# Three-layer graph convolution: comparisons for the count products made five at a time and earlier, more places for count products and matrices, shared chunk rows split once per group

## The chip, the cores and the metric

The kernel runs on one core of a Trainium2 chip. The time is the device time of one execution in microseconds (us). The profile comes from a hardware profiler that recorded one execution of its own. Engines are named as in the profile: PE (TensorE, matrix products; PEld is its loading of the stationary operand), DVE (VectorE), ACT (ScalarE), POOL (GpSimd, which here issues the gathers), SP (SyncE, which issues most other transfers).

## The reference

A graph of 6250 nodes with 256 features and 100000 edges, sorted by destination, goes through three graph convolutions, then a residual sum and a normalisation. Biases are drawn at random, and W1 is scaled by 8. Widths are 256 to 512, 512 to 512 and 512 to 256.

```python
def _gcn_layer(h_in, W, b, src, dst, norm_edge, n_nodes):
    h = h_in @ W
    msg = h[src] * norm_edge[:, None]
    agg = jax.ops.segment_sum(msg, dst, num_segments=n_nodes)
    return agg + b
...
src = jnp.concatenate([edge_index[0], loops])
dst = jnp.concatenate([edge_index[1], loops])
deg = jax.ops.segment_sum(jnp.ones_like(dst, dtype=x.dtype), dst, num_segments=n)
dinv = jnp.where(deg > 0, jax.lax.rsqrt(deg), 0.0)
norm_edge = dinv[src] * dinv[dst]
h = x
for W, b in ((W1, b1), (W2, b2), (W3, b3)):
    h = jax.nn.relu(_gcn_layer(h, W, b, src, dst, norm_edge, n))
return h
...
x = _layernorm(x + _L0_gnn_ref(x, edge_index, ...), axis=-1)
```

All is float32.

## The kernel before

**Blocks, chunks and groups.** The nodes are cut into 50 blocks of Q = 125. A block's incoming edges are taken as KF = 16 *chunks* of 128 edges; what a block has beyond 2048 edges goes into a *shared chunk*, one for each group of GRP = 10 blocks. The sum over edges into a node is done in one of two ways.

*Gathered blocks.* For each chunk an indirect DMA, issued by POOL (L829), brings the 128 source rows from a table in DRAM into a row buffer in `room`. DVE makes a one-hot matrix `shot` (L798; four chunks at a time, by comparing `near_cols`, the numbers 0 to 124 in a PSUM bank, with the edges' destinations), and PE multiplies the two into the block's accumulator `sacc` (L855). Where a chunk is *halved*, its float32 row is first split into a high part (ACT, L870) and a remainder (DVE, L873), `halves`, and goes through PE as one product in the mode float32r; where it is not, it goes as float32. Halved are every second chunk in layer 0, three of four in layer 1, and all in layer 2, but never the shared chunk. The shared chunk's rows are gathered once in a group, and multiplied once for each block, after its sixteenth chunk.

*Dense blocks.* For the first FEW = 18 blocks in layer 0 and the first MANY = 28 in layer 2, no rows are gathered. A matrix of counts (how many edges from each node into each of the block's nodes, one byte each, 125 x 6250) is loaded from the DRAM tensor `kept` into one of two places `used`, widened into `piece` five source blocks at a time (L806), and 50 products with `parts`, the split features of all nodes held in SBUF, give the same sum (L898).

**Counting.** The count matrices are themselves made on the chip by `counts(b)` (L688), 18 in layer 0 and ten in layer 1. It goes through 28 steps; a count product handles G = 5 destination nodes, so there are GB = 25 in a block and 700 in all. For each, DVE compares the numbers in `keys` with one column of `slots` twice: `hot_lo` (L702) marks an edge's place in its source block, `hot_key` (L704) its source block and destination node. Two steps later PE multiplies them into one half of the PSUM tile `mat_ps`, the half alternating (L710), and a step after that ACT copies the counts as bytes into `made` (L694). After the last copy SP stores `made` to `kept` (L713), and there is one `made`:

```python
if u > 2:
    moved(u - 3)
if 1 < u < GB + 2:
    hot_lo, hot_key = hot.pop(u - 2)
    nc.tensor.matmul(mat_ps[:Q, u % 2, :G * NB], lhsT=hot_lo, rhs=hot_key, start=True, stop=True)
if u % rush != rush - 1:
    yield 1
```

`slots` comes from `windows(t)` (L429), six rounds of small products and comparisons, two of them before layer 0.

**Order of the work.** The instructions of each engine run in the order in which the program writes them; waits between engines follow from the tiles that they share, a tile of a pool being taken as a whole. Each layer is a loop over the chunks (L864). One step issues the gather of chunk c, the high split of chunk c - hi_lag, the remainder of c - lo_lag and the product of c - lag, then lets everything else move on by one step: first what finishes a block (`after1`, `after2`, `after3`: scaling, transposing, weight products, bias, relu, store), then `go_fixed` (L877), which advances windows and counting, then as many dense products as an even spread asks for. The lags are in L37:

```python
SPLIT = ((1, 2, 4), (1, 2, 4), (3, 4, 6))
```

A gather may run ahead of its product by as many steps as there are row buffers: of `first_rows` two are kept for shared chunks and 19 rotate in layer 0. Layer 0 has 516 gathers (32 blocks and four groups' shared chunks), layer 1 has 805, layer 2 355. `making_few` (L1059) runs the counting of layer 0: it counts a block, then, when the dense block before the last is finished, fetches the block's matrix into `used`, then counts the next. In layer 1 the ten countings start at fixed, evenly spread chunks. Pools of `halves` have three buffers in layer 0 and four in layers 1 and 2; `pairs`, which holds the hot tiles, has four.

## Time and profile before

| | us |
|---|---|
| median of three executions | 2779.82 |
| lowest and highest | 2773.82, 2794.70 |
| the profiled execution, and its span in the records | 2769.12, 2767.1 |
| clock granted to PE, mean over the span | 0.905 |

The largest groups of instructions, from the page (line, engine, what, how often, busy us, mean ns):

| line | engine and work | count | busy | mean |
|---|---|---|---|---|
| L829 | POOL, gather issue | 1664 | 1650.0 | 992 |
| L855 | PE, gathered product, halved rows | 1808 | 773.3 | 486 |
| L855 | PE, gathered product, unsplit rows | 1120 | 483.9 | 516 |
| L898 | PE, dense product (three places of the sum) | 2300 | 765.0 | |
| L710 | PE, count product | 700 | 203.4 | 291 |
| L873 | DVE, remainder of a split | 1208 | 663.6 | 556 |
| L798 | DVE, `shot` | 443 | 296.3 | 669 |
| L702, L704 | DVE, comparisons | 1400 | 401.7 | 277, 297 |
| L870 | ACT, high part of a split | 1208 | 600.9 | 510 |
| L694 | ACT, copy of counts | 700 | 305.6 | 437 |
| L806 | ACT, `piece` | 376 | 264.9 | 712 |

How to read what is shown further on: the page's first part gives busy time, share of the span and number of instructions per engine; its slices cut the span into 40 parts and give busy tenths; its chain follows the work that ended last back to the start, and "issue" is time in which an engine waited for nothing that the records show. In the view by stage a row begins with the stretch in us from the start of the span. In the view of waits a row names an engine, the tile and line of the instruction that waited, what it is taken to have waited for, then total us, times and the longest. In the timeline a row is start, duration, engine, line and operation with out<-in, and in brackets the idle time ahead of it and what ended it. Records on one engine can overlap, and busy PE time is not PE at its peak.

### The profile page before, as it was taken

How to read it: one execution, taken by the hardware profiler on the slowest of the kernel's cores; microseconds unless marked ns; L12 is line 12 of the kernel's file. 1: busy time of each engine (PE TensorE's matmuls, PEld its weight loads, DVE VectorE, ACT ScalarE, POOL GpSimd, SP SyncE). 2: the span in 40 equal slices, each digit the busy share in tenths (PEclk: the TensorE clock that was granted, in tenths of full speed). 3: DMA queues.
4: the chain of work that ended last, by engine and by line, in shares of the span. 5: the costliest groups of instructions: out<-in, count | busy, mean ns of one | idle time of the engine just before them, and what ended most of it. 6: DMA issues, size and time to landing. Idle time of an engine off the chain costs nothing.

```text
span 2767.1 us, 30455 instructions
## 1 busy us (share of the span) xinstructions
PE 2130.1 (77%) x7965; PEld 1459.2 (53%) x7965; DVE 1512.0 (55%) x3904; ACT 1266.9 (46%) x2777; POOL 1685.0 (61%) x1717
## 2 busy tenths in 40 slices
PE   3367678887878767878778878778787688888886
PEld 2245445555555434545555545545454466666664
DVE  5555445555555355555555555555554255655656
ACT  2445445555555344444444444444444244444443
POOL 2355556666666466667767667676676366566663
PEclk9988889999999888989998889999899789999998
DMA  7344445455445466666767667676676355555553
GB/s 174 92 124 115 134 136 146 123 149 148 126 143 143 123 196 194 203 195 201 211 191 211 186 181 216 195 203 201 182 216 198 98 137 150 142 147 153 151 145 93
DMA packets 178089, 447.70 MB, mean 162 GB/s; under 512 B 43347, under 2 KB 75429, under 8 KB 177904
## 3 DMA queue, kind: packets, MB, share of 16 engines
q0 software_dynamic: 107456, 326.24, 42.1%
q1 hardware_dynamic: 55328, 107.63, 13.5%
q10 hardware_dynamic: 15120, 11.77, 1.7%
q8 instruction: 65, 1.06, 0.2%
q14 instruction: 120, 0.98, 0.1%
HBM read 391.61 MB, written 53.88 MB: 161 GB/s over the span
## 4 chain that ended last, share of the span: by engine, by line
PE 53%; issue 17%; DVE 9%; another core or an unknown queue 7%; ACT 6%; DMA 5%; POOL 3%; ACTq 0%; POOLq 0%; SPq 0%; DVEq 0%
PE sacc L855 20%; PE sacc L898 10%; PE win_ps L985 5%; DMA room<-tab,ssrc 4%; PE win_ps L898 4%; PE mat_ps L898 3%; PE mat_ps L710 3%; PE smm L945 3%; DVE halves L873 3%; ACT halves L870 3%; POOL room L829 2%; PE smm L1002 2%; DVE shot L798 1%; ACT piece L806 1%
## 5 line engine op out<-in xcount | busy, mean ns | idle before, releaser
L829 POOL DMA_INDIRECT room<-tab,ssrc x1664 | 1650.0, 992 | 878.8 <-issue 333.3
L873 DVE TENSOR_TENSOR halves<-room,halves 128x256 fp32r<-128x256 f32 (+1 forms) x1208 | 663.6, 556 | 805.1 <-ACT halves L870 382.7
L855 PE MATMUL sacc<-halves,shot 128*125 128x512 f32 x1808 | 773.3, 486 | 156.0 <-issue 66.0
L870 ACT CAST halves<-room 128x256 fp32r<-128x256 f32 (+1 forms) x1208 | 600.9, 510 | 610.9 <-PE sacc L855 170.0
L855 PEld LDWEIGHTS sacc<-halves,shot 128*125 128x125 f32 x1808 | 349.4, 203 | 494.1 <-issue 289.1
L694 ACT CAST room<-mat_ps 125x250 uint8<-125x250 f32 x700 | 305.6, 437 | 544.2 <-PE mat_ps L710 165.4
L898 PE MATMUL sacc<-parts,piece 125*125 125x512 f32 x1400 | 498.7, 454 | 34.5 <-ACT piece L806 19.4
L855 PE MATMUL sacc<-room,shot 128*125 128x256 f32 (+1 forms) x1120 | 483.9, 516 | 10.6 <-DMA room<-tab,ssrc 10.6
L710 PE MATMUL mat_ps<-hot_key,hot_lo 128*125 128x250 bf16 x700 | 203.4, 291 | 308.3 <-issue 128.5
L898 PEld LDWEIGHTS sacc<-parts,piece 125*125 125x125 f32 x1400 | 254.8, 203 | 274.0 <-issue 196.4
L702 DVE TENSOR_SCALAR hot_lo<-keys,slots 128x125 bf16<-128x125 bf16 x700 | 193.6, 277 | 264.9 <-remote 114.2
L798 DVE TENSOR_TENSOR shot<-near_cols,sdlo 128x500 fp32r<-128x500 f32 x443 | 296.3, 669 | 0.1
L806 ACT CAST piece<-room 125x625 fp32r<-125x625 uint8 x376 | 264.9, 712 | 59.5 <-DVE halves L873 13.0
L855 PEld LDWEIGHTS sacc<-room,shot 128*125 128x125 f32 x1120 | 218.7, 204 | 130.0 <-issue 69.8
L985 PE MATMUL win_ps<-room,w_sb 128*128 128x250 f32 x800 | 218.2, 399 | 6.0 <-ACT room L993 5.3
L704 DVE TENSOR_SCALAR hot_key<-keys,slots 128x250 bf16<-128x250 bf16 x700 | 208.1, 297 | 0.0
L985 PEld LDWEIGHTS win_ps<-room,w_sb 128*128 128x128 f32 x800 | 164.7, 206 | 58.1 <-issue 26.1
L898 PE MATMUL mat_ps<-parts,piece 125*125 125x512 f32 x450 | 132.2, 412 | 16.9 <-ACT piece L806 8.4
L898 PE MATMUL win_ps<-parts,piece 125*125 125x512 f32 x450 | 134.1, 419 | 13.5 <-ACT piece L806 10.3
L710 PEld LDWEIGHTS <-hot_lo 128*125 128x125 bf16 x700 | 104.5, 150 | 60.9 <-issue 24.2
L945 PE MATMUL smm<-w,szt 128*125 128x512 f32 x200 | 110.6, 641 | 1.3 <-DVE st L950 0.6
L1002 PE MATMUL smm<-w,room 128*125 128x256 f32 x400 | 109.0, 398 | 0.0
(174 smaller groups left out, 1246.8 us busy)
## 6 DMA issues: line engine op xcount, KB each, us to landing
room<-kept SPq DMA_DIRECT2D x46, 683.6 KB
room<-tab,ssrc POOLq DMA_INDIRECT x1664
kept<-room SPq DMA_DIRECT2D x28, 683.6 KB
tab<-st SPq DMA_DIRECT2D x75, 224.0 KB
room<-tab SPq DMA_DIRECT2D x50, 224.0 KB
room<-in_x SPq DMA_DIRECT2D x50, 112.0 KB
out<-st ACTq DMA_DIRECT2D x50, 112.0 KB
room<-in_x ACTq DMA_DIRECT2D x4, 1120.0 KB
```

The costliest lines, as they stand in the source:

```text
L694: nc.scalar.copy(made[:, :, u * G:(u + 1) * G], mat_ps[:Q, u % 2, :G * NB].rearrange("p (k r) -> p k r", r=G))
L704: nc.vector.tensor_scalar(hot_key, keys, slots[:, t, 1, w:w + 1], None, op0=ALU.is_equal)
L710: nc.tensor.matmul(mat_ps[:Q, u % 2, :G * NB], lhsT=hot_lo, rhs=hot_key, start=True, stop=True)
L798: nc.vector.tensor_tensor(hot[:, :n], near_cols.unsqueeze(1).to_broadcast([P, n, Q]), dlo.rearrange("p b j -> p (b j)")[:, at:at + n].unsq ...
L806: convert(piece, used[m % 2][:, c * PIECE:(c + 1) * PIECE, :])
L829: nc.gpsimd.indirect_dma_start(out=row, out_offset=None, in_=tables[i], in_offset=bass.IndirectOffsetOnAxis(ap=at, axis=0))
L855: nc.tensor.matmul(acc[:Q, :size], lhsT=hot, rhs=row[:, c0:c0 + size], start=(i == 1 and k == c0 == 0), stop=(k == KF and c0 + size == row ...
L870: nc.scalar.copy(halves[:, :width], landed[chunk - hi_lag])
L873: nc.vector.tensor_sub(halves[:, width:], landed.pop(chunk - lo_lag), halves[:, :width].bitcast(F32))
L898: nc.tensor.matmul(acc_d[:Q], lhsT=got[done // PIECE][:, k % PIECE, :], rhs=parts[:, k], start=False, stop=(k == NB - 1))
L945: nc.tensor.matmul(y_ps, lhsT=zt[:, k, :], rhs=w1_sb[:, k, :], start=(k == 0), stop=(k == KC - 1))
L985: nc.tensor.matmul(h_ps[:, f, :], lhsT=w2_sb[:, k, (f2 + f) * P:(f2 + f + 1) * P], rhs=zt2[:, k, :], start=(k == 0), stop=(k == KH - 1))
```

## The change

- **Comparisons.** `counts` takes a list of blocks and makes the comparisons of WIDE = 5 count products together: one TENSOR_TENSOR for five `hot_lo` and two for five `hot_key` (three columns at one step, two columns two steps later). They read `near_cols`, which now holds the numbers 0 to 249 in float32, and `slots`, now BF16, each spread by broadcasting. `pairs` holds two tiles of five.
- **Count products.** A product comes four steps after the step that starts its five, its copy one step later. Products go in turn to three places: the two halves of `mat_ps`, and columns 256 to 505 of the PSUM bank that also holds `near_cols`.
- **Matrices.** Counting of layer 0 runs on without a break between blocks, 25 steps a block, and fills `made` and a second place `also_made` in turn; the first block still goes at about two products a step. Fetching is a list of steps of its own, and takes a block once its store has been issued. In layer 1 each count of a block has the one place `made`, as before. `also_made` takes the room of six row buffers: 13 rotate in layer 0.
- **Shared chunk.** Its row is split like a halved chunk, once for its group, into a pool of its own with two buffers, and all blocks of the group use these halves.
- **Sizes.** `halves` has four buffers in layer 0 and five in layer 2. `dynamic_dma_scratch_size` is 4096. `thr0` is dropped (`windows` computes it from `cols`), and b3 is loaded between layers 1 and 2, on SP, into a tile made there, rather than before layer 0.

The diff, without the lines that move b3 and without what is unchanged:

```diff
-    slots = const.tile([P, NW, 2, Q], F32, name="slots")
+    slots = const.tile([P, NW, 2, Q], BF16, name="slots")
...
     cols = const.tile([P, P], F32, name="scols")
-    thr0 = const.tile([P, Q], F32, name="thr0")
...
         thr = scratch[:P, 0:125]
-        nc.vector.tensor_single_scalar(thr, thr0, float(G * Q * t), op=ALU.add)
+        nc.vector.tensor_scalar(thr, cols[:, :Q], float(G), float(G * Q * t), op0=ALU.mult, op1=ALU.add)
...
-    made, *used = [room[:Q, n * MW:(n + 1) * MW].bitcast(U8)[:, :NB * Q].rearrange("p (k v) -> p k v", v=Q) for n in range(3)]
-    first_rows = [room[:, at:at + C] for at in range(3 * MW, room.shape[1] - C + 1, C)]
+    made, *used, also_made = [room[:Q, n * MW:(n + 1) * MW].bitcast(U8)[:, :NB * Q].rearrange("p (k v) -> p k v", v=Q)
+                              for n in range(4)]
+    first_rows = [room[:, at:at + C] for at in range(4 * MW, room.shape[1] - C + 1, C)]
...
-    pairs = early.enter_context(tc.tile_pool(name="spairs", bufs=4))
+    pairs = early.enter_context(tc.tile_pool(name="spairs", bufs=2))
...
-    split = one.enter_context(tc.tile_pool(name="sfirst_split", bufs=3))
+    split = one.enter_context(tc.tile_pool(name="sfirst_split", bufs=4))
+    shared_split = one.enter_context(tc.tile_pool(name="sfirst_shared", bufs=2))
...
-    near_cols = ps_cols.tile([P, 512], F32, name="near_cols")[:, :Q]
-    nc.vector.tensor_copy(near_cols, cols[:, :Q])
+    near = ps_cols.tile([P, 512], F32, name="near_cols")
+    near_cols = near[:, :G * NB]
+    nc.vector.tensor_copy(near_cols, keys)
+    mat_places = [mat_ps[:Q, 0, :G * NB], mat_ps[:Q, 1, :G * NB], near[:Q, 256:256 + G * NB]]
...
-    def counts(b, rush=GB + 3):
-        def moved(u):
-            nc.scalar.copy(made[:, :, u * G:(u + 1) * G],
-                           mat_ps[:Q, u % 2, :G * NB].rearrange("p (k r) -> p k r", r=G))
+    def counts(blocks, places, rush=0):
+        def compared(out, numbers):
+            shape = list(out.shape)
+            nc.vector.tensor_tensor(out, near_cols[:, :shape[2]].unsqueeze(1).to_broadcast(shape),
+                                    numbers.unsqueeze(2).to_broadcast(shape), op=ALU.is_equal)
         hot = {}
-        for u in range(GB + 3):
-            if u < GB:
-                t, w = divmod(b * GB + u, Q)
-                hot_lo = pairs.tile([P, Q], BF16, name="hot_lo")
-                nc.vector.tensor_scalar(hot_lo, hot_cols[:, :Q], slots[:, t, 0, w:w + 1], None, op0=ALU.is_equal)
-                hot_key = pairs.tile([P, G * NB], BF16, name="hot_key")
-                nc.vector.tensor_scalar(hot_key, keys, slots[:, t, 1, w:w + 1], None, op0=ALU.is_equal)
-                hot[u] = hot_lo, hot_key
-            if u > 2:
-                moved(u - 3)
-            if 1 < u < GB + 2:
-                hot_lo, hot_key = hot.pop(u - 2)
-                nc.tensor.matmul(mat_ps[:Q, u % 2, :G * NB], lhsT=hot_lo, rhs=hot_key, start=True, stop=True)
-            if u % rush != rush - 1:
+        total = len(blocks) * GB
+        for s in range(total + 5):
+            if s < total and s % GB == 0:
+                while (blocks[s // GB] + 1) * GB > seen * Q:
+                    yield 1
+            if s < total and s % WIDE == 0:
+                t, w = divmod(blocks[s // GB] * GB + s % GB, Q)
+                hot_lo = pairs.tile([P, WIDE, Q], BF16, name="hot_lo")
+                hot_key = pairs.tile([P, WIDE, G * NB], BF16, name="hot_key")
+                hot[s // WIDE] = hot_lo, hot_key
+                compared(hot_lo, slots[:, t, 0, w:w + WIDE])
+                compared(hot_key[:, :3], slots[:, t, 1, w:w + 3])
+            if s < total and s % WIDE == 2:
+                t, w = divmod(blocks[s // GB] * GB + s % GB + 1, Q)
+                compared(hot[s // WIDE][1][:, 3:], slots[:, t, 1, w:w + WIDE - 3])
+            m = s - 4
+            if 0 <= m < total:
+                hot_lo, hot_key = [h[:, m % WIDE] for h in hot[m // WIDE]]
+                nc.tensor.matmul(mat_places[m % 3], lhsT=hot_lo, rhs=hot_key, start=True, stop=True)
+            m = s - 5
+            if 0 <= m:
+                n, u = divmod(m, GB)
+                place = places[n % len(places)]
+                nc.scalar.copy(place[:, :, u * G:(u + 1) * G], mat_places[m % 3].rearrange("p (k r) -> p k r", r=G))
+                if u == GB - 1:
+                    by_rows(nc.sync, place.rearrange("p k v -> p (k v)"), kept[blocks[n]], store=True)
+                    stored.append(blocks[n])
+            if s >= rush or s % 2:
                 yield 1
-        by_rows(nc.sync, made.rearrange("p k v -> p (k v)"), kept[b], store=True)
     there = []
     finished = 0
+    stored = []
     def fetch(b, chunk):
         by_rows(nc.sync, used[len(there) % 2].rearrange("p k v -> p (k v)"), kept[b])
         there.append(chunk)
-    hot_cols = keys
...
                 hot = onehot.tile([P, HOTS, Q], F32R, name="shot")
-                nc.vector.tensor_tensor(hot[:, :n], near_cols.unsqueeze(1).to_broadcast([P, n, Q]),
+                nc.vector.tensor_tensor(hot[:, :n], near_cols[:, :Q].unsqueeze(1).to_broadcast([P, n, Q]),
...
         landed, split_rows = {}, {}
+        group_rows = None
...
         def halved(c):
-            return 0 <= c < total and items[c][1] is not None and (i == 2 or items[c][2] % (2, 4)[i] > 0)
+            return 0 <= c < total and (items[c][1] is None or i == 2 or items[c][2] % (2, 4)[i] > 0)
...
                 row, at = shared[n % 2], rest[:, n, 0:1]
             else:
                 row, at = rows[turn % len(rows)], src[:, b, j:j + 1]
-                landed[c] = row
                 turn += 1
+            landed[c] = row
...
         def product(c):
             nonlocal acc
+            nonlocal group_rows
             n, b, j = items[c]
             if b is None:
+                group_rows = split_rows.pop(c)
                 return
...
             several = [(j, split_rows.pop(c) if halved(c) else landed.pop(c))]
             if j == KF - 1:
-                several.append((KF, shared[b // GRP % 2]))
+                several.append((KF, group_rows))
...
                 if halved(chunk - hi_lag):
-                    halves = split_rows[chunk - hi_lag] = split.tile([P, 2 * width], F32R, name="halves")
+                    pool, name = (split, "halves") if items[chunk - hi_lag][1] is not None else (shared_split, "shared")
+                    halves = split_rows[chunk - hi_lag] = pool.tile([P, 2 * width], F32R, name=name)
                     nc.scalar.copy(halves[:, :width], landed[chunk - hi_lag])
...
-    def making_few():
+    def fetching_few():
         for m, b in enumerate(few):
-            while (b + 1) * GB > seen * Q:
-                yield 1
-            yield from counts(b) if m else counts(b, 2)
-            while finished < m - 1:
+            while b not in stored or finished < m - 1:
                 yield 1
             fetch(b, now + 10)
     first = 28
     spacing = (steps(FEW) - first - 12) / FEW
-    layer(0, C, every[FEW:], few, after1, first_rows, first, spacing, [(0, all_windows()), (1, making_few())])
+    layer(0, C, every[FEW:], few, after1, first_rows, first, spacing, [(0, all_windows()), (1, counts(few, (made, also_made), GB)), (1, fetching_few())])
...
     split = two.enter_context(tc.tile_pool(name="swide_split", bufs=4))
+    shared_split = two.enter_context(tc.tile_pool(name="swide_shared", bufs=2))
...
-          extras=[(5, last_weights())] + [(10 + gap * n, counts(b)) for n, b in enumerate(many[FEW:])])
+          extras=[(5, last_weights())] + [(10 + gap * n, counts([b], (made,))) for n, b in enumerate(many[FEW:])])
...
-    split = ctx.enter_context(tc.tile_pool(name="ssplit", bufs=4))
+    split = ctx.enter_context(tc.tile_pool(name="ssplit", bufs=5))
+    shared_split = ctx.enter_context(tc.tile_pool(name="sshared", bufs=2))
...
-    nc = bacc.Bacc("TRN2", target_bir_lowering=False, num_devices=1)
+    nc = bacc.Bacc("TRN2", target_bir_lowering=False, num_devices=1, dynamic_dma_scratch_size=4096)
```

## The prediction

> **What bounds the kernel now.** I read the page first (engines, slices, chain), then busy time by stage, then who waited for whom in each stage, and last a stretch of the timeline.
>
> ```profile
> PE 2130.1 (77%) x7965; PEld 1459.2 (53%) x7965; DVE 1512.0 (55%) x3904; ACT 1266.9 (46%) x2777; POOL 1685.0 (61%) x1717
> ...
> PEclk9988889999999888989998889999899789999998
> ...
> PE 53%; issue 17%; DVE 9%; another core or an unknown queue 7%; ACT 6%; DMA 5%; POOL 3%; ACTq 0%; POOLq 0%; SPq 0%; DVEq 0%
> ```
>
> The reader is to see that TensorE (PE) is the busiest engine and more than half of the chain, but idle for 637 us, and that a quarter of the chain is nobody's work ("issue", "unknown queue"). The clock row never stays at full speed: it falls after idle stretches. By stage:
>
> ```profile
> core 0: us, PE busy (x) PEld busy (x) DVE busy (x) ACT busy (x) POOL busy (x), PEclk, DMA share, GB/s
> 0.00:100.00 100.00, 32.47 (x197) 26.14 (x197) 55.71 (x138) 34.60 (x64) 18.89 (x38) 1.00 0.64 157
> 100.00:931.00 831.00, 639.28 (x2528) 444.56 (x2529) 434.60 (x1460) 423.69 (x1025) 501.01 (x520) 0.90 0.46 132
> 931.00:953.00 22.00, 13.44 (x45) 7.06 (x43) 7.41 (x15) 6.49 (x15) 0.46 (x1) 1.00 0.23 71
> 953.00:2190.00 1237.00, 965.28 (x3352) 621.01 (x3353) 679.49 (x1414) 540.25 (x1077) 823.14 (x810) 0.89 0.68 195
> 2190.00:2767.00 577.00, 479.61 (x1845) 360.43 (x1844) 334.75 (x878) 261.87 (x597) 341.48 (x351) 0.91 0.52 138
> ```
>
> The stages are preparation, layer 0 (516 gathers, so 1.61 us a step), a handover, layer 1 (805, 1.54 us) and layer 2 (355, 1.63 us). In layer 0 PE idles 192 us. The waits of PE in 100 to 931 us (total us, times, longest):
>
> ```profile
> PE mat_ps L710 <- issue: 60.8, 30, 6.9
> PE mat_ps L710 <- DVE hot_key L704: 53.5, 26, 13.8
> PE mat_ps L710 <- ACT room L694: 45.0, 31, 5.9
> PE mat_ps L710 <- DVE hot_lo L702: 15.6, 16, 3.0
> ```
>
> Nearly all of it, 174.9 us in 103 waits, stands ahead of one instruction, the count product L710. In 953 to 2190 us the same line has 67.7 + 21.8 + 21.7 + 5.2 + 4.2 = 120.6 us. Whom the tool names differs, but the program's waits are plain: each L710 waits for the L694 copy of the product just before it (`mat_ps` is tracked as one tile, so its two halves do not help), and that copy waits for that product. PE to ACT and back, once a step. The timeline shows what this does:
>
> ```profile
> 218.78 0.37 PE L710 MATMUL mat_ps<-hot_key,hot_lo 128*125 128x250 bf16 x1 [2.01 <-issue]
> ...
> 223.93 0.44 ACT L694 CAST room<-mat_ps 125x250 uint8<-125x250 f32 x1 [4.63 <-remote]
> 223.93 0.34 DVE L702 TENSOR_SCALAR hot_lo<-keys,slots 128x125 bf16<-128x125 bf16 x1 [5.18 <-remote]
> ...
> 224.42 0.37 PE L710 MATMUL mat_ps<-hot_key,hot_lo 128*125 128x250 bf16 x1 [3.99 <-ACT room L694]
> ```
>
> The product at 218.78 lasts 0.37 us, yet its copy and a comparison that waits for it both start at 223.93: PE's answer came 4.8 us late. Why, the trace does not say; whatever has no slack pays for it in full. A second cause: there is one `made`, so the first copy of a block waits until the last block's store has landed. ACT's waits in layer 0:
>
> ```profile
> ACT room L694 <- remote: 106.2, 24, 12.9
> ...
> ACT room L694 <- DMA kept<-room: 40.2, 10, 5.5
> ```
>
> Ten are named, 4.0 us each; there are 17 such block changes.
>
> **The change, part by part.** The sum is against the profiled execution (span 2767.1, 2769.1 us); the median of the runs shown is 10.7 us above it, added at the end.
>
> (a) Shared rows split once. 54 products in layers 0 and 2 were two f32 passes of 408 ns each and become one of 486: 54 × 330 ns = 17.8 us. 50 in layer 1 were 2 × 651 and become 2 × 486: 16.5 us. Added are 12 splits (ACT 404 or 618 ns, DVE 423 or 691), beside idle ACT and DVE. On the path I count layers 0 and 2 in full and half of layer 1: **−26**.
>
> (b) `also_made`. The 17 waits vanish in layer 0, about 3 us of PE idle each (4.0 less what PE still had): **−50**. SP's stores and loads are as many as before.
>
> (c) Products and copies. In the new program the two products into `mat_ps` wait for copies two and three products back (one wait serves both); the third, in the `near` bank, for the copy three back. Slack goes from one step to two or three. Left of L710's waits is 125 us in layer 0, mean 1.7 us; two more steps are 2.5 us of PE work (639/516 = 1.24 us a step), so most of a wait is covered. But late answers come in rows, and one product in three hangs on DVE (f). I take half in layer 0, **−62**. In layer 1 half is 60, and POOL presses there (823 busy + 810 × 0.30 us between gathers = 1066 of 1237), so **−40**. Counting also takes 25 steps a block instead of 28, which spreads dense products; no further gain taken.
>
> (d) Comparisons. Five columns were ten TENSOR_SCALAR; now three TENSOR_TENSOR of 625, 750 and 500 elements, reading `near_cols` in PSUM. From the subtraction rows (256: 423 ns, 512: 691 ns) an element is 1.05 ns and the rest 155 ns: 809 + 940 + 670 (the measured `shot` of 500) = 2.42 us. Before, by rows, 5 × (277 + 297) = 2.87 us, but the records overlap:
>
> ```profile
> 205.51 0.25 DVE L702 TENSOR_SCALAR hot_lo<-keys,slots 128x125 bf16<-128x125 bf16 x1
> 205.68 0.27 DVE L704 TENSOR_SCALAR hot_key<-keys,slots 128x250 bf16<-128x250 bf16 x1
> ...
> 205.88 0.24 DVE L702 TENSOR_SCALAR hot_lo<-keys,slots 128x125 bf16<-128x125 bf16 x1
> ```
>
> 0.37 us a pair, 1.85 us for five; the new three with 0.1 us of overlap each make 2.13. So over 140 fives −63 to +39 us of DVE. [...]
>
> (e) Layer 2 gets five `halves` instead of four. Its ACT splits wait 68.0 + 30.0 + 25.9 + 16.9 us for PE, and PE 36.1 us for DVE `halves` in turn: **−20**. Layer 0's fourth goes with (c). Fewer idle stretches also keep the clock up: layer 0 at 0.90 has about 20% of its time at half speed, and a quarter of that saved over 639 us of work is some 15 us: **−15**.
>
> (f) New waits. `near_cols` and the third place are one tile. So each third product waits for the last DVE read of it (a `shot` or comparison), and the next DVE read waits for that product and its copy; behind the waiting DVE stand the `halves` subtractions that PE wants. No row shows it. Round trip per three products: product 0.3 + copy 0.44 + gaps 0.3, and up to two steps of DVE at 435/516 = 0.84 us, in bad places a 1.75 us pair plus about 1.7 us more: 2.7 to 4.5 us, against 3 × 1.24 = 3.7 of PE work. Bounds: 0, and 0.8 us for all 233 round trips, 186 us. By the DVE load nearer the low end: **+35**.
>
> (g) Layer 0's rotating rows fall from 19 to 13, so gathers run nine steps ahead of their product instead of fifteen: some 11 to 14 us. The longest gather wait in layer 0 is 7.9 us. Between 0 and 30: **+10**. [...] BF16 `slots`, the dropped `thr0` and the late `b3` are a handful of instructions and one DMA on SP at the start of layer 2, ahead of a first use several steps later: zero.
>
> Sum: −26 − 50 − 62 − 40 − 20 − 15 + 35 + 10 = −168; 2769 − 168 + 11 = **2612 us**.
>
> **Rivals.** *Late answers pass through.* If PE's answers come late in rows and the third place hands them on, (c) and the clock fail: 2780 − 26 − 50 − 20 + 45 = 2729. For it: clusters, as between 213 and 232 us. Against: most waits are under 2.5 us.
> *The shared bank decides (slower).* If the round trip PE, ACT, DVE, PE of (f) takes longer than three steps of today, 3 × 1.61 = 4.83 us, layer 0 gains nothing. At 5.8 us its 150 trips cost +145, less 26 and 20: 2780 + 99 = 2879. For it: a comparison pair of 1.75 us in one step. Against: DVE's 0.84 us a step.
> *All slack is found.* L710's waits go almost entirely, and layer 2 follows: −26 − 55 − 110 − 85 − 30 − 25 + 30 = −301, about 2480. For it: L710 is nearly PE's only wait in layer 0. Against: gathers alone, at 1.25 us each, need 645 us of layer 0.
>
> **How the numbers follow.** Forecast 0.66 (2550 to 2690), pass-through 0.14, shared bank 0.08, all slack 0.12. The range 2530 to 2755 leaves out the slow case, half of the fastest and a few hundredths of the rest, some 0.19. Within 1% of 2780 (2752 to 2808) is about what a measurement of this kernel cannot tell from no change. Faster: 0.66 + 0.12 + most of 0.14, less the forecast's tail, 0.85; same 0.06; slower 0.09.
>
> **What would show it.** In the new profile: PE's idle before the count product in layer 0 well under 100 us, with few `kept` stores among ACT's waits; layer 0 near 720 us, layer 1 near 1190, layer 2 near 550; unsplit products gone from layer 2; gathers as long as now. Wrong would be: long waits of DVE's reads of `near_cols` or of each third product, or POOL waiting for rows while ACT waits for landings.

## The result and the profile after

The changed kernel took 2753.06 us (four runs, 2749.66 to 2761.23) beside 2784.90 us for the kernel before: a ratio of 0.987, 95% interval 0.9827 to 0.9913. It is faster beyond its interval, but by 32 us, where 168 were forecast. Repeated beside the kernel before on two more occasions it gave 0.9829 (0.9805 to 0.9852) and 0.9851 (0.9818 to 0.9884).

One thing has to be known to read what follows. The runs went to several chips of the same type, and these fall into two kinds. On kind A (the first comparison and two later sets of runs) the kernel before takes 2785 to 2796 us; on kind B (three sets, each on a chip of its own) it takes 2351 to 2353 us. Each kernel was timed beside the kernel before on the same chip, so ratios hold; microseconds are compared only within a kind. On kind B the changed kernel is slower: 1.0074 (1.005 to 1.0098).

From the page of the changed kernel (first comparison, kind A), engines, clock and chain:

```profile
PE 2108.5 (76%) x7911; PEld 1444.9 (52%) x7911; DVE 1544.8 (56%) x2935; ACT 1247.0 (45%) x2789; POOL 1683.6 (61%) x1716
...
PEclk9889999999998788998998998889889789999998
...
PE 38%; issue 15%; DVE 8%; ACT 7%; another core or an unknown queue 7%; DMA 4%; POOL 1%; SPq 1%; ACTq 0%; DVEq 0%; POOLq 0%
```

The view by stage, cut here at the first and last gather of each layer (columns as in the prediction), shows layers 0, 1 and 2:

```profile
core 0: us, PE busy (x) PEld busy (x) DVE busy (x) ACT busy (x) POOL busy (x), PEclk, DMA share, GB/s
...
98.70:896.40 797.70, 621.62 (x2507) 427.39 (x2508) 457.24 (x840) 412.64 (x1035) 504.40 (x519) 0.92 0.48 138
...
918.20:2137.10 1218.90, 943.50 (x3272) 606.58 (x3272) 687.02 (x1057) 530.73 (x1067) 814.65 (x805) 0.88 0.67 195
...
2171.30:2733.80 562.50, 464.45 (x1796) 356.16 (x1797) 319.80 (x841) 252.31 (x582) 345.27 (x354) 0.91 0.53 141
```

Cut in the same way, the kernel before had 833.4, 1197.3 and 558.4 us. So layer 0 gave 36 us and the other two gave nothing; their differences are those of one execution to the next, as the further profiles show (last table of the experiments). PE worked 17 us less in layer 0 and was idle 19 us less. What PE waited for in layer 0 (98 to 897 us; total us, times, longest):

```profile
PE near_cols L722 <- DVE hot_key L700: 35.6, 30, 4.3
PE mat_ps L722 <- ACT room L727: 22.5, 15, 4.9
PE szt_ps L944 <- ACT szt L962: 16.8, 6, 5.8
...
PE sacc L921 <- ACT room L727: 8.0, 1, 8.0
PE sacc L921 <- ACT piece L825: 7.4, 2, 4.7
PE smm L968 <- DVE st L973: 7.3, 4, 2.6
```

Before, nearly every wait stood ahead of the count product. Now transposes (L944), weight products (L968) and dense products (L921) wait too. Summing every gap between PE's records by the instruction that ends it:

| PE idle, us | before (2 profiles) | changed (3 profiles) |
|---|---|---|
| layer 0, ahead of count products | 178, 187 | 99, 99, 99 |
| layer 0, ahead of all else | 22, 20 | 83, 90, 82 |
| layer 1, ahead of count products | 130, 129 | 125, 116, 105 |
| layer 1, ahead of all else | 132, 136 | 155, 157, 160 |
| layer 2 | 92, 98 | 102, 98, 94 |

The reader is to see that the waits aimed at did go, 84 us of them in layer 0, and that 64 us came back ahead of other instructions.

### The profile page after: what moved, and what is told of

It is laid out like the page before. It is cut to its first block, busy times and chain, and to the rows that moved or that the text cites. A ratio compares the mean times of both kernels' runs of the same rounds, so it can differ in the third digit from the quotient of the medians.

```text
span 2759.6 us, 29575 instructions
## 1 busy us (share of the span) xinstructions
PE 2108.5 (76%) x7911; PEld 1444.9 (52%) x7911; DVE 1544.8 (56%) x2935; ACT 1247.0 (45%) x2789; POOL 1683.6 (61%) x1716
## 4 chain that ended last, share of the span: by engine, by line
PE 38%; issue 15%; DVE 8%; ACT 7%; another core or an unknown queue 7%; DMA 4%; POOL 1%; SPq 1%; ACTq 0%; DVEq 0%; POOLq 0%
PE sacc L877 15%; PE sacc L921 6%; PE win_ps L1008 4%; PE win_ps L921 4%; DMA room<-tab,ssrc 3%; ACT halves L893 3%; DVE halves L896 3%; PE mat_ps L921 3%; PE smm L1025 2%; PE smm L968 2%; DVE hot_key L700 1%; ACT piece L825 1%; DVE shot L817 1%; POOL room L849 1%
## 5 line engine op out<-in xcount | busy, mean ns | idle before, releaser
L921 PE MATMUL sacc<-parts,piece 125*125 125x512 f32 x1400 | 504.6, 452 | 56.0 <-ACT piece L825 40.9
L877 PE MATMUL sacc<-room,shot 128*125 128x256 f32 (+1 forms) x912 | 402.3, 525 | 14.7 <-DMA room<-tab,ssrc 13.2
L921 PEld LDWEIGHTS sacc<-parts,piece 125*125 125x125 f32 x1400 | 252.2, 202 | 175.2 <-issue 72.7
L727 ACT CAST room<-mat_ps 125x250 uint8<-125x250 f32 x470 | 197.8, 438 | 296.6 <-PE mat_ps L722 129.8
L700 DVE TENSOR_TENSOR hot_key<-near_cols,slots 128x750 bf16<-128x750 f32 (+1 forms) x280 | 224.2, 801 | 43.5 <-PE mat_ps L722 14.4
L877 PEld LDWEIGHTS sacc<-room,shot 128*125 128x125 f32 x912 | 180.0, 208 | 75.6 <-issue 27.3
L722 PE MATMUL mat_ps<-hot_key,hot_lo 128*125 128x250 bf16 x470 | 136.9, 294 | 76.8 <-ACT room L727 46.6
L727 ACT CAST room<-near_cols 125x250 uint8<-125x250 f32 x230 | 100.8, 438 | 207.6 <-DVE hot_key L700 87.5
L722 PE MATMUL near_cols<-hot_key,hot_lo 128*125 128x250 bf16 x230 | 70.5, 307 | 147.0 <-DVE hot_key L700 64.6
L921 PE MATMUL win_ps<-parts,piece 125*125 125x512 f32 x450 | 134.6, 419 | 20.7 <-ACT piece L825 17.7
L921 PE MATMUL mat_ps<-parts,piece 125*125 125x512 f32 x450 | 131.2, 411 | 23.4 <-ACT piece L825 23.1
L700 DVE TENSOR_TENSOR hot_lo<-near_cols,slots 128x625 bf16<-128x625 f32 x140 | 113.1, 808 | 55.0 <-PE mat_ps L722 14.8
```

What stands on the lines that cost most here:

```text
L700: nc.vector.tensor_tensor(out, near_cols[:, :shape[2]].unsqueeze(1).to_broadcast(shape), numbers.unsqueeze(2).to_broadcast(shape), op=ALU. ...
L722: nc.tensor.matmul(mat_places[m % 3], lhsT=hot_lo, rhs=hot_key, start=True, stop=True)
L727: nc.scalar.copy(place[:, :, u * G:(u + 1) * G], mat_places[m % 3].rearrange("p (k r) -> p k r", r=G))
L877: nc.tensor.matmul(acc[:Q, :size], lhsT=hot, rhs=row[:, c0:c0 + size], start=(i == 1 and k == c0 == 0), stop=(k == KF and c0 + size == row ...
L921: nc.tensor.matmul(acc_d[:Q], lhsT=got[done // PIECE][:, k % PIECE, :], rhs=parts[:, k], start=False, stop=(k == NB - 1))
```

## The experiments

**Which kind of chip, and who sets the pace.** The kernel before, and the changed one, unchanged.

> The kernel before, unchanged, for its profile on the chip of these runs, since times of the kernel before differ by 18% between the first comparison (2785 us) and the first four runs (2351 us). If the difference is that PE reports its finished products late on the chip of the first comparison, then a chip with 2351 us shows layer 0 near 672 us, hardly a wait of PE for records that name nobody, and gathers back to back at 1.25 us; a chip with 2785 us shows layer 0 near 833.

> The changed kernel, unchanged, beside the kernel before on the chip of these runs. If the gathers' issue sets the pace (1676 x 1.25 us = 2101 us of some 2350) and the bank shared by third place and numbers costs what layer 0 of the run without counts in layer 1 showed against two places (688 against 665 us), the ratio is 0.998 to 1.008 on a chip with 2351 us. If the slack of three places is worth anything there, it is below the 0.9926 of two places. On a chip with 2785 us it is 0.983 to 0.991 as in the first comparison.

> The changed kernel, unchanged, beside the kernel before on the chip of these runs; on a chip where the kernel before takes about 2351 us it has not been measured. If the third place beside the numbers costs what layer 0 shows there (688 and 692 us with it, 663 to 665 without), the ratio is 1.001 to 1.008, slower than with two places (0.992). If the slack is worth something, it is below 0.992. On a chip with 2790 us 0.983 again.

> The changed kernel, unchanged, for the other kind of chip, should it come up: on a chip with 2351 us 1.001 to 1.008 if the bank shared with the numbers costs what layer 0 of two other kernels with three places shows there, 0.992 or less if it does not. On a chip with 2790 us 0.984 again.

Measured: c0 on kind A, 2793.43 us, layer 0 838 us, as in the first profile. c1 0.9829 and f1 0.9851 on kind A; h1 on kind B 1.0074, layer 0 689 us. POOL's timeline in layer 0 of the kernel before (kind A) shows the pace:

```profile
608.44 0.95 POOL L829 DMA_INDIRECT room<-tab,ssrc  x1 [2.24 <-PE mat_ps L710]
609.69 0.95 POOL L829 DMA_INDIRECT room<-tab,ssrc  x1 [0.30 <-issue]
610.95 0.94 POOL L829 DMA_INDIRECT room<-tab,ssrc  x1 [0.30 <-PE mat_ps L710]
612.20 0.95 POOL L829 DMA_INDIRECT room<-tab,ssrc  x1 [0.30 <-issue]
613.45 0.95 POOL L829 DMA_INDIRECT room<-tab,ssrc  x1 [0.30 <-issue]
614.70 0.94 POOL L829 DMA_INDIRECT room<-tab,ssrc  x1 [0.30 <-issue]
617.38 0.95 POOL L829 DMA_INDIRECT room<-tab,ssrc  x1 [1.74 <-DVE hot_lo L702]
```

Gathers go out back to back, 1.25 us apart; an idle time of 0.30 is only the gap between two of them, whoever is named. 69% of those in layer 0 start within 1.27 us of the one before. A layer is its gathers times the median spacing (1.254 us) plus what the longer spacings have over it. For layer 0 of the kernel before that is 516 x 1.254 = 647, plus 186, together 833 us; the changed kernel has 647 + 151 = 798. The 186 us are 131 of POOL waiting for a row beyond the ordinary 0.30, 40 of POOL waiting ahead of four other gathers, and some 11 of gathers that themselves took longer. The four others fetch edges for `windows`, at places that DVE has to work out first. Their row among POOL's waits in layer 0, before, and in the changed kernel (f1):

```profile
POOL w_sb L459 <- DVE hot_lo L702: 41.5, 4, 11.7
```

```profile
POOL w_sb L462 <- DVE w_sb L459: 14.9, 4, 5.1
```

The waits for rows are 122 to 132 us in the three profiles of the changed kernel, beside 131 and 135 before. So most of what layer 0 gained shows ahead of these four gathers; that is its place, not yet its cause.

The same program on both kinds of chip (f3 and e4 below are one kernel) tells what the excess is. POOL's waits in layer 0, kind A:

```profile
POOL room L831 <- issue: 89.3, 281, 1.9
POOL room L831 <- PE sacc L859: 64.1, 52, 3.7
POOL room L831 <- PE mat_ps L711: 59.4, 42, 5.2
```

and kind B:

```profile
POOL room L831 <- issue: 59.4, 195, 0.3
...
POOL room L831 <- PE mat_ps L711: 16.8, 55, 0.3
POOL room L831 <- PE sacc L859: 16.1, 43, 1.5
```

On kind B hardly a gather waits beyond the ordinary 0.30. On kind A POOL waits up to 5.2 us for PE. Taking all instructions of ACT and DVE in layer 0 that wait for PE and for no transfer, and matching each with its product by the program's order: on kind A 140 of 934 start more than 0.5 us after both the product's recorded end and their own engine's last work (299 us in all), on kind B 15 of 935 (14 us). In layer 1 it is 187 of 727 against 11 of 731. So PE's late answers, which the prediction saw in one place, belong to kind A and reach waiters of every sort. The two profiles of this one kernel differ by 434 us (2786.7 and 2352.5), and POOL's waits beyond the ordinary 0.30, summed over the layers, by 428 of them (433 and 4). That POOL waits longer because of the late answers fits, but PE also works slower on kind A: it is busy 2112.8 us there and 1993.8 on kind B, at a granted clock of 0.899 and 0.933. No run tells the two apart.

An instance from the changed kernel in layer 2, where nothing is counted. ACT's timeline, with the idle time ahead in brackets:

```profile
2475.26 0.71 ACT L825 CAST piece<-room 125x625 fp32r<-125x625 uint8 x1
2475.87 0.40 ACT L893 CAST halves<-room 128x256 fp32r<-128x256 f32 x1
2476.95 0.78 ACTq L54 DMA_DIRECT2D out<-st  x2
2481.98 0.71 ACT L825 CAST piece<-room 125x625 fp32r<-125x625 uint8 x1 [5.71 <-remote]
```

and PE's:

```profile
2473.97 1.32 PE L921 MATMUL mat_ps<-parts,piece 125*125 125x512 f32 x5
...
2479.30 0.39 PE L921 MATMUL mat_ps<-parts,piece 125*125 125x512 f32 x1
```

The `piece` at 2481.98 takes over the buffer whose last reader is a product of the first row, recorded as over by 2475.29. The answer came 6.7 us later, and PE, out of pieces after 2479.69, stood until 2482.75. The trace names nobody ("remote").

**One part of the change left out, kind A.** `e5`: one place for matrices. `e6`: two places for count products, one of them beside the numbers.

```diff
-    layer(0, C, every[FEW:], few, after1, first_rows, first, spacing, [(0, all_windows()), (1, counts(few, (made, also_made), GB)), (1, fetching_few())])
+    layer(0, C, every[FEW:], few, after1, first_rows, first, spacing, [(0, all_windows()), (1, counts(few, (made,), GB)), (1, fetching_few())])
```

```diff
-    mat_places = [mat_ps[:Q, 0, :G * NB], mat_ps[:Q, 1, :G * NB], near[:Q, 256:256 + G * NB]]
+    mat_places = [mat_ps[:Q, 0, :G * NB], near[:Q, 256:256 + G * NB]]
```

> The changed kernel with one place made for the matrices of layer 0, so that the first copy of a block waits again for the store of the block before. The prediction took 50 us for the second place: 50 us slower than the changed kernel, all in layer 0. If PE's waits only matter where they make POOL wait for a row, 15 us or less.

> The changed kernel with two places for count products, one half of mat_ps and the place beside the numbers: every second product, not every third, shares the bank that DVE reads, and each product waits for the copy two products back. If the shared bank is what costs (layer 0 is 22 us longer with one product in three there than with none, on a chip with 2351 us), layer 0 is another 8 to 15 us longer than that of the changed kernel. If it is the order or number of steps and not the bank, it is within 5 us of the changed kernel.

Measured: e5 2790.62 us, 0.9992 (0.9973 to 1.0012), which is 39 us more than c1 in the same set, with layer 0 at 849 against 806 us and POOL's waits for rows there at 178 against 132. Inside the changed kernel the second place is worth 39 of the 50 us forecast, and without it the rest of the change is worth nothing. e6 0.9848 (0.9819 to 0.9877), layer 0 804 us: half of the products in the shared bank cost no more there than a third, which is the second of the two outcomes expected.

**Two places for count products instead of three.** `e1` and `d1` are the same kernel; `g1` has 19 rotating rows in layer 0 as well.

```diff
-    mat_places = [mat_ps[:Q, 0, :G * NB], mat_ps[:Q, 1, :G * NB], near[:Q, 256:256 + G * NB]]
+    mat_places = [mat_ps[:Q, 0, :G * NB], mat_ps[:Q, 1, :G * NB]]
```

> The changed kernel with two places for count products (the halves of mat_ps) instead of three: each product waits again for the copy of the product just before it, and DVE's reads of near_cols share their bank with no product. If the slack of the three places is worth what the prediction took (62 us in layer 0, 40 in layer 1, less 35 for the shared bank), this is 60 to 75 us slower than the changed kernel, 2813 to 2828 us. If PE's answers come late for everyone and the slack only moved PE's wait from the count product to other instructions, it is within 25 us of the changed kernel, 2735 to 2780 us, and the waits ahead of the count product rise by 50 us or more while those ahead of transposes, weight products and gathered products fall by as much. If the shared bank took back all that the slack gained, it is 0 to 30 us faster.

> The changed kernel with two places for count products, run again to have it on the other kind of chip. On a chip with 2790 us: if the slack of three places is worth what the prediction took, 60 to 75 us slower than the changed kernel, ratio 1.005 to 1.010; if PE's late answers only find another waiter, within 15 us of it, ratio 0.979 to 0.989. On a chip with 2351 us 0.993 again.

> The changed kernel with two places for count products, nothing of PE's beside the numbers, and also_made in a tile of its own, so that 19 rows rotate in layer 0. On a chip with 2351 us rows are no limit: 0.988 to 0.994, as with two places alone. On a chip with 2790 us: below 0.976 if rows or the shared bank take something there, 0.979 to 0.987 if neither does, above 0.995 if the slack of three places was worth what the prediction took.

Measured, kind B: e1 0.9926 (0.9897 to 0.9955) and d1 0.9917 (0.9897 to 0.9936), against 1.0074 with three places: the third place costs 1.5%, some 35 us, 24 to 26 of them in layer 0 (689 against 665 and 663). Kind A: g1 0.9945 (0.9922 to 0.9968), 31 us slower than f1 in the same set (2780.49 against 2749.25), layer 0 828 against 804 us, layer 1 equal (1203 and 1203).

On kind A the 24 us of layer 0 cannot be put down to the slack alone. Eighteen of them arose in its first 200 gathers, while `windows` was at work (344 us in g1, 326 in f1); the other 316 took 484 and 478 us, and PE idled 87 and 89 us in them. POOL's four edge gathers waited 43.4 us in g1 and 14.9 in f1, and its waits for rows are equal (128 and 129). In the nine profiles of kind A these four waits come to 41 to 43 us where 19 rows rotate and to 14 or 15 where 13 do, and no kernel run there had 13 rows without a place beside the numbers. So the rows are a rival of the slack here that no run excludes.

On kind B the third place costs more than it brings. PE's waits in layer 0 there tell why, first with three places (h1), then with two (d1):

```profile
PE near_cols L722 <- DVE hot_key L700: 44.4, 39, 3.1
...
PE near_cols L722 <- DVE shot L817: 7.3, 8, 1.9
...
PE mat_ps L722 <- ACT room L727: 2.4, 4, 1.1
```

```profile
PE mat_ps L722 <- ACT room L727: 16.6, 30, 2.5
PE smm L968 <- DVE st L973: 14.9, 18, 3.0
```

With three places the product beside the numbers waits 52 us for DVE's reads of that bank; with two, 17 us for ACT's copy. On kind B, where 15 of 935 answers were late (e4), the handshake that the third place removes costs less than the one it adds.

**Numbers in SBUF, so that nothing of DVE's is in the bank of the third place.**

```diff
-    near_cols = near[:, :G * NB]
+    near_cols = const.tile([P, G * NB], F32, name="near_sb")
```

> The changed kernel with the numbers 0 to 249 in a tile of their own in SBUF, so that comparisons and shot no longer read the bank of the third place. If the shared bank decides (every third product waiting for DVE, DVE waiting for it and its copy), PE's waits ahead of the near_cols product, 66 us in layer 0 and 77 in layer 1, fall by half or more and the time by 30 to 70 us, to 2680 to 2725 us. If PE's late answers decide, those waits turn up elsewhere and the time stays within 15 us of the changed kernel, 2738 to 2768 us.

Measured, kind B: 1.0359 (1.0332 to 1.0386), some 67 us above the changed kernel there, neither of the two. The waits on the bank went, but the gathers got longer; POOL's group in e2 and in the changed kernel (h1), two kernels that differ in nothing else:

```profile
L849 POOL DMA_INDIRECT room<-tab,ssrc x1664 | 1750.1, 1052 | 507.4 <-issue 233.7
```

```profile
L849 POOL DMA_INDIRECT room<-tab,ssrc x1664 | 1636.6, 984 | 537.0 <-issue 245.7
```

With POOL as the pace, 113 us more of its work show in the time. So this run does not tell what the bank costs.

**Counting in layer 1 left out** (`work=False` skips comparisons, products and copies of `counts` there, so ten matrices of layer 2 are not the reference's).

> The changed kernel with the counting of layer 1 left out: no comparisons, count products and copies there (250 products), so the ten matrices made in layer 1 are not the reference's; their stores and loads stay. By the prediction's reading, in which PE's work and its waits ahead of count products lie on the path of layer 1, PE's 74 us of products and 123 us of waits go and layer 1 falls by 130 to 200 us, to 1020 to 1090. If layer 1 is bound by the gathers' ring of rows, it falls by less than 25 us. If late answers pass from one waiter to the next, it falls by about the products' own time, 50 to 90 us.

Measured, kind B: 0.9999 (0.9982 to 1.0015), 18 us below the changed kernel there; layer 1 1042 against 1056 us. 250 products with all their waits are worth 14 us of layer 1, as a layer bound by its gathers would have it: 805 x 1.251 = 1007.

**Shared rows alone, second place alone** (parts of the change made in the kernel before; the code is that of the change), **and 19 rows** (the changed kernel with `also_made` in a tile of its own).

```diff
-    first_rows = [room[:, at:at + C] for at in range(4 * MW, room.shape[1] - C + 1, C)]
+    also_made = const.tile([P, MW], F32, name="also_made")[:Q].bitcast(U8)[:, :NB * Q].rearrange("p (k v) -> p k v", v=Q)
+    first_rows = [room[:, at:at + C] for at in range(3 * MW, room.shape[1] - C + 1, C)]
```

> The kernel before with only the shared chunk's rows split once per group (and the scratch of 4 KB, which makes room). The prediction took 26 us: 2750 to 2765 us. If PE's idle time simply grows by what PE saves, it is within 10 us of the kernel before. If the new split lands in the way of other splits on ACT and DVE, it is 5 to 20 us slower.

> The kernel before with only the shared rows split once, run again to have it on the other kind of chip. On a chip with 2790 us: 26 us faster, ratio 0.991, if PE's work lies on the path as the prediction took it; 0.997 to 1.003 if PE's saved time turns into idle time. On a chip with 2351 us 1.000 again.

> The kernel before with only the shared rows split once. On a chip with 2790 us, where it has not been measured: 0.991 if PE's work lies on the path as the prediction took it (26 us), 0.997 to 1.003 if PE's saved time turns into idle time. On a chip with 2351 us 1.000 as in two runs.

> The kernel before with only the second place for matrices in layer 0, used in turn (and so 13 rotating rows there instead of 19); pairs of comparisons, 28 steps a block and two places for count products stay. On a chip where the kernel before takes about 2790 us: if the second place is the whole gain of the change, as one made against two suggests (2791 against 2752), this alone gives 0.980 to 0.990 of the kernel before, and ACT's waits for the stores of kept go. If it pays only together with the free-running counting and the slack, it gives less than 15 us, 0.995 or more. On a chip with 2351 us, where POOL waits for rows only 24 us in layer 0, it gives 0.995 to 1.002.

> The kernel before with only the second place for matrices. On a chip with 2790 us, where it has not been measured: 0.995 to 0.999 (3 to 14 us) if the wait for the store and the wait of product for copy stand in one row, so that removing one leaves the other; 0.986 or less if the second place is the gain by itself. On a chip with 2351 us 0.996 again.

> The changed kernel with also_made in a tile of its own, so that 19 rows rotate in layer 0 instead of 13. If the fewer rows make POOL wait (its waits for rows in layer 0 of the changed kernel come to 160 us on a chip with 2790 us), layer 0 falls by 15 to 40 us and the ratio is 0.968 to 0.978 there. The prediction took 10 us: 0.979. If rows are no limit, 0.983 as the changed kernel. On a chip with 2351 us it is 5 us or less.

> The changed kernel with also_made in a tile of its own and so 19 rotating rows in layer 0. On a chip with 2790 us: the prediction took 10 us for the missing rows, so 0.980 against 0.984; if rows are what POOL lacks (158 us of its waits in layer 0), 0.975 or less; if the answer that frees a row is late however many rows there are, 0.982 to 0.987. On a chip with 2351 us 1.004 again, and within 3 us of the changed kernel.

Measured: shared rows alone 0.9993 (0.9968 to 1.0018) on kind A and 1.0005 (0.9988 to 1.0023) on kind B, where a repetition, d4, gave 0.9998 (0.9983 to 1.0012). On kind A PE's busy time fell from 2137.8 us (c0; 2130.1 in the first profile) to 2112.8, which is 17 to 25 of the 34 us of PE work that the prediction saw go (it took 26 of them as time), and the time did not fall. Second place alone 0.9961 (0.9945 to 0.9976) and, repeated as h3, 0.9968 (0.9953 to 0.9983), both on kind B; on kind A it was not run. 19 rows 1.0043 (1.0026 to 1.006) and, as h2, 1.0041 (1.0025 to 1.0057), on kind B; the changed kernel in the same set as h2 had 1.0074, so the six rows are worth 4 to 8 us there (medians 2362.70 and 2366.62), hardly beyond the intervals. On kind A they were not run alone.

From the first to the last gather of each layer, us, one figure for each profile:

| | kind A: layer 0 | layer 1 | layer 2 | kind B: layer 0 | layer 1 | layer 2 |
|---|---|---|---|---|---|---|
| gathers x spacing | 647 | 1010 | 445 | 646 | 1007 | 444 |
| before | 833, 838 | 1197, 1211 | 558, 567 | | | |
| before, shared rows once | 831 | 1214 | 560 | 672, 669 | 1058, 1063 | 457, 458 |
| before, second place | | | | 670, 671 | 1050, 1051 | 458, 458 |
| changed | 798, 806, 804 | 1219, 1205, 1203 | 563, 563, 557 | 689 | 1056 | 456 |
| changed, one made | 849 | 1204 | 557 | | | |
| changed, two places | | | | 665, 663 | 1050, 1047 | 459, 458 |
| changed, two places, 19 rows | 828 | 1203 | 567 | | | |
| changed, two places, one beside the numbers | 804 | 1211 | 562 | | | |
| changed, 19 rows | | | | 692, 680 | 1057, 1056 | 457, 458 |

Layers 1 and 2 hardly answer to any kernel of this table: layer 1 stays within 1197 and 1219 us on kind A, 1047 and 1063 on kind B. In layer 0 on kind A no part brings its gain alone: 849 without the second place, 828 with it but with two count places and 19 rows, 803 with all, beside 836 before. On kind B two places for count products are faster than both kernels; on kind A, with 19 rows, they are slower than three with 13. No run here is the best on both.

## Why the prediction was wrong

On kind A the direction was right and the size was not; on kind B the direction was wrong too. By its own steps, on kind A unless said:

- **(a) shared rows, -26: nothing** (0.9993). PE's work fell by 17 to 25 us, but the step "on the path" was wrong: PE's idle time ahead of its products in layer 0 grew instead, to 214 us from 200 and 208.
- **(b) `also_made`, -50: 39 us**, 42 in layer 0. The mechanism was right and the size near. But it was added to the others as if independent, and on kind A it was measured only inside the changed kernel.
- **(c) slack, -62 in layer 0 and -40 in layer 1: at most 24 us and nothing** (g1 beside f1, net of the shared bank, and with six rows more in g1). This is the step that failed: "Left of L710's waits is 125 us in layer 0 ... I take half". The sum took a wait of PE that goes for time that goes. With the whole change, the waits ahead of the count product in layer 0 fell by 84 us, and 64 us reappeared ahead of other products, as PE's answers come late to those who feed them too (140 of 934 in layer 0 of f3). In the gathers after `windows` was done PE idled no less (88, 94 and 89 us beside 86 and 91 before). In layer 1 the count product still waits 105 to 125 us with three places, and 88 with two (g1).
- **(d) comparisons, 0: right in what was measured.** 808, 928 and 673 ns were measured for the three against an estimated 809, 940 and 670, and DVE's busy time rose by 33 us (1512.0 to 1544.8), within the estimated -63 to +39. The sum has no term for them; that DVE's idle time takes up the 33 us no run shows, as none had the comparisons alone.
- **(e) layer 2's fifth buffer, -20, and the clock, -15: nothing.** Layer 2 took 558 and 567 before, 563, 563 and 557 after. The granted clock went from 0.905 to 0.899; in layer 0 it was 0.90 and 0.89 before and 0.92, 0.91 and 0.90 after, in layer 1 0.90 and 0.89 before and 0.88 after.
- **(f) shared bank, +35: 35 us on kind B** (0.992 against 1.0074), net of what the slack brings there; h1's 52 us of waits ahead of the third place fit. On kind A it is inside the 24 us of (c) and cannot be told from it: e6, with more of it, was no slower.
- **(g) fewer rows, +10: 4 to 8 us on kind B**; not measured alone on kind A, where fewer rows may even have helped (the rival in (c)). The sum has nothing for the scratch of 4 KB: no run had it alone, and the three with it and the shared rows gave 0.9993, 1.0005 and 0.9998 (f3, e4, d4).

Two rivals were nearer than the forecast. "Late answers pass through" gave 2729 and is what happened on kind A; it still counted 46 us of gains in shared rows and layer 2 that did not come, so that it lay only 24 us too low is in part luck. On kind A it should have been the likeliest, since the prediction had the 4.8 us instance in its own timeline and let it stand as one clustered stretch. "The shared bank decides" is what happened on kind B, at 35 of the 145 us that it named. The sentence that held the key stood in the third rival as an argument against: gathers alone need 645 us of layer 0. POOL's excess, 186, 187 and 113 us in the three layers, bounds what each could lose; the forecast lay within it, so this sum alone would not have refuted it. The row of the four edge gathers (41.5 us) would have shown one place where layer 0 could gain.

Left open: why PE's answers are late on kind A. There the trace also loses records: of the 4250 semaphore updates that PE makes in the kernel with shared rows, kind A recorded 3136 and kind B 4242, and of the landings of gathers 7174 against 27113. No run here was made without records, and none shows whether the lost ones and the late answers have one cause. It was not settled. Also not tried: 13 rows with both count places in `mat_ps` on kind A, which would tell rows from slack, and a third place in a bank that nobody else reads.

## What to carry to other kernels

Before adding up an engine's waits, find the instruction that paces the loop (here 1.25 us a gather, to be seen as a constant distance of starts) and sum only what lies above count times spacing; a wait that goes elsewhere is worth only what leaves that excess. Two profiles compared at the same gather number show in which part of a layer a gain arose; here that was the part where a second user of POOL waited. When an answer is late for no reason that the trace names, ask whether all waiters see such answers; if so, a buffer for one of them may only move the wait to the next. And a place borrowed in a bank that another engine reads ties two engines by whole-tile tracking: weigh that new handshake (here 52 us of PE's waits in layer 0 on kind B) against the one it removes (17).

## What the runs showed of the hardware

- Chips of one type differed by 18 to 19% in the time of one program (2785 to 2796 against 2351 to 2353 us). Between the two profiles of one kernel (f3 and e4) the traces show late answers of PE (140 of 934 in layer 0 against 15 of 935), a granted clock of 0.899 against 0.933 with PE busy 119 us longer, and lost records (3136 of PE's 4250 updates recorded against 4242). On kind A, PE's recorded updates come in steps: beyond 1.2 us the most frequent distances are about 1.42, 2.13 and 2.84 us, multiples of 0.71.
- A product's recorded end was 6.7 us ahead of the moment at which its waiter went on (the changed kernel on kind A, in layer 2); in layer 0 on kind B the usual distance was 0.04 us.
- Moving the numbers that DVE compares from PSUM to SBUF made 168 of layer 0's 516 gathers longer than 1.1 us (e2), against 19 with the numbers in PSUM (h1), with the median at 949 and 946 ns.
- In the records of the kernel before the granted clock is either full or one half, and 177 of its 178 stretches last a multiple of 3.41 us, the shortest 3.41. In layer 0 each of 27 drops to one half followed 3.4 us in which PE was busy at most 47%, 30% on average. In layer 1 the same stretch had up to 61%, so no limit can be read from this.
